# Upper half of z's rows by Strassen, first steps of the running sums on ScalarE

## The chip, the cores and the metric

One core of a Trainium2 chip. The time is device microseconds of one execution, the median over runs; what is compared is this time before and after the change. TensorE is called PE (its weight loads PEld), VectorE DVE, ScalarE ACT, GpSimd POOL, and SyncE SP. SP issues most transfers, POOL the indirect ones. Every engine executes its own list of instructions in order; waits between engines are semaphores.

## The reference

There are 32 batches of x, 512 channels by 1024 columns, float32, and one 512×512 matrix adj.

```python
# layer 0
q = wq . x;  k = wk . x                        # (B, N) each
att = softmax(leaky(q[:, None, :] + k[:, :, None]), axis=-1)   # slope 0.01
agg = einsum('bcn,bmn->bcm', x, att)
x = layernorm(x + relu(adj @ agg + bm))
# layer 1
W = adj * adj
x = layernorm(x + einsum('bnf,nm->bmf', x, W) + bias)
```

Both layernorms run over the last axis, 1024 elements.

## The kernel before, in words

**Layer 0.** The attention is not formed. A score is leaky(q_n + k_m), so for a given m the columns n fall into two sets by whether q_n exceeds −k_m, and in each set the weight is a product of a factor of q_n and one of k_m. The kernel therefore sorts the columns by q and takes running sums of z = xᵀ·adjᵀ (1024 rows of 512, one row per column n) with one weight upwards and another downwards. Each m then needs only one row of both tables, picked by its count.

In steps for batch b, with the words of the order lists: load x (`ld`); q and k rows by a small product (`parts` L223, copied by `parts_copy` L231, turned by `cols` L238); q's row goes to DRAM and back to all partitions (`row_out`, `row` L259); `row_max` (`rc`, L265); `rank` (`rk`, DVE, L275, 8 per batch) and `count` (`ct`, ACT, L288, 8 per batch). `product` (`z`, L314) makes 128 rows of z: for each j of 8, four matmuls of 128×128 by 128×512 into one PSUM bank; `product_copy` (`zc`, ACT, L320) takes them to `zt`, and `scatter` (`sc`, POOL, L328) writes them to sorted rows in DRAM. `sums_load` (`sl`) brings eight sorted rows to each partition, `sums_exp` (`se`, L352) makes the weights, `up` (`u`, L361 for j = 0, L366 after) and `down` (`d`, L374 for j = 7, L376 after) are the running sums on DVE, `carry` (`cu`, `cd`, L384) sums over partitions on PE with copies on ACT (L391), `table_up` and `table_down` (`tu`, `td`, L409) add the carries, and `table_write` (`tw`) writes the table to DRAM. `gather` (`g`, POOL, L436) picks rows, `mix_weights` (`mw`, L449), `mix_scale` (`ms`, ACT, L458) and `mix` (`mx`, DVE, L463) form the mean, `turn` (`t`, PE, L487) transposes it to channels by columns, and `residual` (`r`, DVE, L495) adds it to x. `spread0` (`s0`, ACT, L473), `root0`, `root0_end` (`rce`) and `norm0` (`n0`, ACT, L513) normalize the four channel tiles of x in place.

**Layer 1** is a product of the 512×512 matrix (adj∘adj plus the identity) with x, done for the quarters of both by the Strassen-Winograd form with seven products for eight. Sums of the matrix's quarters, S1 to S4, are made once in `weights` on POOL (L173–177). Sums of x's quarters are `T1` to `T4` (`t1`–`t4`, DVE, L524–538). The products are `U`, `V`, `Y`, `Z`, `C11`, `C12`, `C21` (PE, L545 and L580), two rows of tiles each; a running sum in one PSUM bank is copied out between them (`Uc`, `Vc`, `Zc`) and added back at the end (`upper` L600, `lower_right` L606, `lower_left` L613). `U` begins with a short pass that brings in the bias (L543). Then come the second normalization and the `store` (`st`).

**Buffers.** Four x tiles are in flight (`xp`). PSUM has four single banks (pool `p1`: z, q and k rows, carries, the sums of layer 1) and two pairs (pool `p2`: transposes, layer 1's pairs). `qb`, q's row on all partitions, has two buffers; the outputs `g` of layer 1 have four.

**Order.** The schedule is written by hand: three lists of words, `op.batch.index`, are emitted in order, and each engine gets its instructions in that order. `head` covers the start, `loop` is one period, in which one batch is in the products of z, the next in the running sums, one in the gathers and one in layer 1 (used for 15 values of b), `tail` covers the end. The framework adds semaphore waits where tiles or buffers overlap. A PSUM bank is one unit for it: a reader waits for all writes to the bank that were issued before it.

## Time and profile before

| | |
|---|---|
| median of 3 runs | 2003.04 us (2000.26 to 2005.85) |
| the profiled execution, own time | 2002.69 us |
| its span | 2001.0 us |
| mean granted PE clock | 0.988 |
| steady period (from U of one batch to U of the next) | 59.88 us |
| first U (layer 1 of batch 0) starts | 149.43 us |
| U of batch 28 starts | 1822.18 us |
| DMA, mean over the span | 279 GB/s |

The profile is of one execution. A line of the page's groups gives the code line, engine and operation, output and input by the program's names, and the count, then the busy time and the mean duration in ns; a line of the timeline gives start and length in us, and in brackets the idle time just before it and what ended it. Successive instructions overlap by a little, so durations add to more than the elapsed time; the rate of a run of equal instructions is read from the starts. A float32 matmul is recorded as two passes.

### The profile page before, as it was taken

Reading aid. Unit: us, or ns where it says so; the run is one execution under the profiler, and the core shown is the slowest. Engines: PE = TensorE matmul, PEld = TensorE weight load, DVE = VectorE, ACT = ScalarE, POOL = GpSimd, SP = SyncE. Lnnn points to the kernel's source line nnn. Section 1 sums busy time; section 2 is a strip of 40 time slices with the busy share of each in tenths; the row PEclk is TensorE's granted clock in tenths of the full one; section 3 lists DMA queues with packets and bytes.
Section 4 is the critical chain, followed back from the end, with each engine's and each line's share of the span. In section 5 each row is a group of like instructions: output and inputs, shape, how many; then the busy total and the mean of one; then the engine's idle time right before and its main releaser. Section 6 shows DMA issues by size and latency. Waiting matters only on the chain.

```text
span 2001.0 us, 21793 instructions
## 1 busy us (share of the span) xinstructions
PE 1937.7 (97%) x6353; PEld 939.7 (47%) x6353; DVE 1683.9 (84%) x2748; ACT 1512.4 (76%) x2560; POOL 870.7 (44%) x1090
## 2 busy tenths in 40 slices
PE   8979999999999999999999999999999999999866
PEld 4434444444444444444444444444444444444332
DVE  5888898898888888888888888888888889889662
ACT  3567788787788877788877788887778888777656
POOL 4333544434553434554444454444454443444331
PEclk9999999999999999999999999999999999999978
DMA  6677777877777877777877777877777877776742
GB/s 226 243 275 295 279 306 273 321 287 279 290 295 290 326 268 273 292 290 295 322 270 279 289 288 295 318 269 278 295 280 298 318 283 276 300 277 257 282 190 85
DMA packets 142832, 557.94 MB, mean 279 GB/s; under 512 B 15044, under 2 KB 15184, under 8 KB 134520
## 3 DMA queue, kind: packets, MB, share of 16 engines
q1 hardware_dynamic: 85328, 354.38, 46.7%
q0 software_dynamic: 57344, 202.15, 26.0%
q8 instruction: 50, 0.82, 0.2%
q14 instruction: 70, 0.57, 0.1%
q10 hardware_dynamic: 40, 0.02, 0.0%
HBM read 287.07 MB, written 269.42 MB: 278 GB/s over the span
## 4 chain that ended last, share of the span: by engine, by line
PE 78%; DVE 7%; DMA 7%; ACT 3%; issue 2%; POOL 2%; SPq 0%; POOLq 0%; DVEq 0%; ACTq 0%
PE z_ps L314 36%; PE sum_ps L545 18%; PE pair_ps L545 9%; PE pair_ps L580 4%; PE agg_ps L487 4%; PE qk_ps L223 3%; DMA got<-table,of 2%; DVE tab L409 2%; DMA tab<-sorted_z 1%; DMA sorted_z<-zt,to 1%; DVE junk_v L275 1%; PE carry_ps_False L384 1%; PE carry_ps_True L384 1%; ACT junk L473 1%; DVE x L495 1%
## 5 line engine op out<-in xcount | busy, mean ns | idle before, releaser
L314 PE MATMUL z_ps<-adj_t,x 128*128 128x512 f32 x2048 | 906.6, 594 | 0.0
L314 PEld LDWEIGHTS z_ps<-adj_t,x 128*128 128x128 f32 x2048 | 379.5, 190 | 444.8 <-issue 430.4
L436 POOL DMA_INDIRECT got<-table,of x256 | 289.7, 1132 | 467.1 <-PE z_ps L314 142.3
L328 POOL DMA_INDIRECT sorted_z<-zt,to x256 | 276.6, 1081 | 293.5 <-ACT zt L320 202.0
L275 DVE SCALAR_TENSOR_TENSOR junk_v<-qb,qkc,tie 128x1024 uint8<-128x1024 f32 x256 | 328.8, 1284 | 5.9
L288 ACT ACTIVATE junk_s<-qb,qkc 128x1024 uint8<-128x1024 f32 x256 | 294.0, 1148 | 6.0 <-DMA qb<-q_row 1.5
L636 ACT ACTIVATE g<-g,nb,tv 128x1024 f32<-128x1024 f32 x128 | 158.6, 1239 | 105.6 <-POOL nb L630 104.9
L320 ACT COPY zt<-z_ps 128x512 f32<-128x512 f32 x256 | 146.8, 577 | 91.2 <-PE z_ps L314 84.2
L480 POOL TENSOR_SCALAR tv<-tv 128x1 f32<-128x1 f32 x128 | 65.4, 511 | 333.1 <-ACT junk L473 330.3
L463 DVE SCALAR_TENSOR_TENSOR got<-got,w 128x512 f32<-128x512 f32 x256 | 184.3, 748 | 28.4 <-ACT got L458 28.3
L473 ACT ACTIVATE junk<-g,tv 128x1024 uint8<-128x1024 f32 x128 | 146.8, 1147 | 81.1 <-DVE g L600 51.1
L458 ACT ACTIVATE got<-got,w 128x512 f32<-128x512 f32 x256 | 165.9, 713 | 50.2 <-DVE w L453 49.9
L473 ACT ACTIVATE junk<-x,tv 128x1024 uint8<-128x1024 f32 x128 | 147.0, 1148 | 44.7 <-DVE x L495 39.4
L495 DVE SCALAR_TENSOR_TENSOR x<-agg_ps,small,x 128x1024 f32<-128x1024 f32 x128 | 161.0, 1280 | 18.5 <-PE agg_ps L487 18.5
L376 DVE SCALAR_TENSOR_TENSOR tab<-tab,ac 128x513 f32<-128x513 f32 x224 | 167.6, 748 | 0.4
L545 PE MATMUL sum_ps<-x,adj 128*128 128x512 f32 x256 | 129.0, 628 | 28.2 <-ACT x L513 28.2
L366 DVE SCALAR_TENSOR_TENSOR tab<-tab,ac 128x514 f32<-128x514 f32 x192 | 144.4, 752 | 12.3 <-ACT ac L352 7.9
L409 DVE TENSOR_TENSOR tab<-tab,carry 128x2052 f32<-128x2052 f32 x64 | 146.6, 2292 | 4.2 <-ACT carry L391 3.9
L487 PEld LDWEIGHTS agg_ps<-ident,got 128*128 128x128 f32 x1024 | 119.2, 143 | 40.4 <-issue 24.5
L513 ACT ACTIVATE x<-x,tv 128x1024 f32<-128x1024 f32 x128 | 136.5, 1136 | 2.0 <-DVE tv L509 1.9
L487 PE MATMUL agg_ps<-ident,got 128*128 128x128 f32 x1024 | 129.7, 277 | 7.3 <-DVE x L495 7.3
L409 DVE TENSOR_TENSOR tab<-tab 128x1539 f32<-128x1539 f32 x64 | 129.5, 2025 | 0.1
(119 smaller groups left out, 2606.4 us busy)
## 6 DMA issues: line engine op xcount, KB each, us to landing
table<-tab SPq DMA_DIRECT2D x64, 2056.0 KB
tab<-sorted_z SPq DMA_DIRECT2D x64, 1028.0 KB
x<-in_x_dram SPq DMA_DIRECT2D x128, 512.0 KB
out_dram<-g SPq DMA_DIRECT2D x128, 512.0 KB
qb<-q_row SPq DMA_DIRECT2D x32, 512.0 KB
sorted_z<-zt,to POOLq DMA_INDIRECT x256, 5.3
got<-table,of POOLq DMA_INDIRECT x256, 8.2
adj_in<-in_adj_dram SPq DMA_DIRECT2D x1, 1024.0 KB
```

Of the source, the lines that this page charges most:

```text
L275: nc.vector.scalar_tensor_tensor(junk, s.qb, s.q[:, j : j + 1], tie[:, at : at + N], ALU.subtract, ALU.is_gt, accum_out=s.rank[:, j : j + 1],)
L288: nc.scalar.activation(junk, s.qb, AF.Sign, bias=s.k[:, j : j + 1], accum_out=s.sign[:, j : j + 1])
L314: nc.tensor.matmul(s.z[j], xt[:, c, j * P : (j + 1) * P], adj_t[:, c, :], start=(c == 0), stop=(c == CT - 1),)
L328: nc.gpsimd.indirect_dma_start(out=sorted_z[b % 2][:, :], out_offset=bass.IndirectOffsetOnAxis(ap=s.to[:, j : j + 1], axis=0), in_=zt[:, j ...
L376: nc.vector.scalar_tensor_tensor(v, v, c, s.zs[:, j + 1, 0:D], ALU.mult, ALU.add)
L409: nc.vector.tensor_tensor(v, v, c, ALU.add)
L436: nc.gpsimd.indirect_dma_start(out=s.got[:, j, :], out_offset=None, in_=table[b % 2][:, :], in_offset=bass.IndirectOffsetOnAxis(ap=s.of[:, ...
L463: nc.vector.scalar_tensor_tensor(up, up, s.w[:, 0, j : j + 1], down, ALU.mult, ALU.add)
L473: nc.scalar.activation(junk, t, AF.Square, bias=v[0][:, i : i + 1], scale=-float(N), accum_out=v[1][:, i : i + 1],)
L487: nc.tensor.transpose(s.agg[o][:, j * P : (j + 1) * P], s.got[:, j, o * P : (o + 1) * P], ident)
L495: nc.vector.scalar_tensor_tensor(t[:, o, :], s.agg[o], nbm[:, o : o + 1], t[:, o, :], ALU.max, ALU.add, accum_out=s.v0[0][:, o : o + 1],)
L545: nc.tensor.matmul(ps, a[:, k, g * P : (g + 1) * P], v[:, k, :], start=False, stop=(k == 1), skip_group_check=first is None,)
```

## The change

Rows 0 to 511 of z (j = 0 to 3) are made as before. Rows 512 to 1023 are made by the Strassen-Winograd form of the 512×512 by 512×512 product xᵀ·adjᵀ: of the quarters of x's right half, x1 to x4 are four sums on DVE (128×512 elements each), R1 to R4 are the matching sums of adjᵀ's quarters, made once on POOL after S1 to S4. Seven products of 256×256 by 256×256 follow: zU, z11, zZ, zV, z12, zY, z21, each for k = 0 and 1, each two matmuls of 128×128 by 128×256. So 28 matmuls of 256 columns stand for 16 of 512.

The running sum z_sum of both k lies in one `p1` bank, 256 columns each; z_pair takes one `p2` buffer. Between the products ACT copies parts to `zt` (zUc, zVc, zZc, and z_lower_left, `zll`: eight copies of 128×256), and DVE adds PSUM to them (z_upper, `zup`, 128×512, twice; z_lower_right, `zlr`, 128×256, twice).

The first step of `up` and the first of `down` move from DVE to ACT. To make room, x1 to x4 share the buffers of layer 1's g_2 and g_3; `qb` has one buffer; the rank's throw-away output shares `end`; `part` and `carry` have one buffer of their own; T2, T3 and T4 lie in `zt` rows 0 to 1, 4 to 5 and 6 to 7. So z's rows j = 0 and 1 stay in PSUM until T4 is read. All three order lists are new; `head` now reaches to batch 12, and `loop` is used for 11 values of b.

```diff
-    op = ctx.enter_context(tc.tile_pool(name="op", bufs=CT))
+    op = ctx.enter_context(tc.tile_pool(name="op", bufs=1))
...
+    B11, B12 = adj_t[:, 0:2, 0:Q], adj_t[:, 0:2, Q:C]
+    B21, B22 = adj_t[:, 2:4, 0:Q], adj_t[:, 2:4, Q:C]
+    R1, R2, R3, R4 = [const.tile([P, 2, Q], F32, name=f"R{i}") for i in (1, 2, 3, 4)]
...
         nc.gpsimd.tensor_scalar(minus_A22, A22, -1.0, None, ALU.mult)
+        nc.gpsimd.tensor_tensor(R1, B12, B11, ALU.subtract)
+        nc.gpsimd.tensor_tensor(R2, B22, R1, ALU.subtract)
+        nc.gpsimd.tensor_tensor(R3, B22, B12, ALU.subtract)
+        nc.gpsimd.tensor_tensor(R4, B21, R2, ALU.subtract)
...
-        s.qb = sp.tile([P, N], F32, tag="qb", name=f"qb_{b}")
+        s.qb = one.tile([P, N], F32, tag="qb", name=f"qb_{b}")
...
+    def x_quarters(b):
+        t = xts[b]
+        return t[:, 0:2, H : H + Q], t[:, 2:4, H : H + Q], t[:, 0:2, H + Q : N], t[:, 2:4, H + Q : N]
+    def x_sums(b, i):
+        s, m = st[b], 2 + i // 2
+        if m not in s.xs:
+            t = op.tile([P, N], F32, tag=f"g{m}", name=f"x_sums_{b}_{m}")
+            s.xs[m] = t.rearrange("p (i k n) -> p i k n", i=2, k=2)
+        return s.xs[m][:, i % 2]
+    def x1(b):
+        _, _, X21, X22 = x_quarters(b)
+        nc.vector.tensor_tensor(x_sums(b, 0), X21, X22, ALU.add)
+    def x2(b):
+        nc.vector.tensor_tensor(x_sums(b, 1), x_sums(b, 0), x_quarters(b)[0], ALU.subtract)
+    def x3(b):
+        X11, _, X21, _ = x_quarters(b)
+        nc.vector.tensor_tensor(x_sums(b, 2), X11, X21, ALU.subtract)
+    def x4(b):
+        nc.vector.tensor_tensor(x_sums(b, 3), x_quarters(b)[1], x_sums(b, 1), ALU.subtract)
+    def z_quarter(ps, a, v, k, start, own):
+        for i in range(2):
+            nc.tensor.matmul(
+                ps, a[:, i, k * P : (k + 1) * P], v[:, i, :], start=start and i == 0,
+                stop=(i == 1), skip_group_check=not own,
+            )
+    def z_sum(b, k):
+        return st[b].zsum[:, k * Q : (k + 1) * Q]
+    def zU(b, k):
+        s = st[b]
+        start = s.zsum is None
+        if start:
+            s.zsum = p1.tile([P, C], F32, tag="m", name=f"z_sum_ps_{b}")
+        z_quarter(z_sum(b, k), x_quarters(b)[0], B11, k, start, start)
+    def zU_copy(b, k):
+        nc.scalar.copy(zt[:, 4 + k, 0:Q], z_sum(b, k))
+    def zV(b, k):
+        z_quarter(z_sum(b, k), x_sums(b, 1), R2, k, False, False)
+    def zV_copy(b, k):
+        nc.scalar.copy(zt[:, 4 + k, Q:C], z_sum(b, k))
+    def zY(b, k):
+        z_quarter(z_sum(b, k), x_sums(b, 2), R3, k, False, False)
+    def z11(b, k):
+        s = st[b]
+        if s.zpair is None:
+            s.zpair = p2.tile([P, N], F32, tag="w", name=f"z_pair_ps_{b}")
+        z_quarter(z_pair(b, k, 0), x_quarters(b)[1], B21, k, True, True)
+    def zZ(b, k):
+        z_quarter(z_pair(b, k, 1), x_sums(b, 0), R1, k, False, False)
+    def z12(b, k):
+        z_quarter(z_pair(b, k, 1), x_sums(b, 3), B22, k, False, False)
+    def z_upper(b, k):
+        v = zt[:, 4 + k, 0:C]
+        nc.vector.tensor_tensor(v, z_pair(b, k), v, ALU.add)
+    def z_lower_right(b, k):
+        v = zt[:, 6 + k, Q:C]
+        nc.vector.tensor_tensor(v, z_sum(b, k), v, ALU.add)
+    def z21(b, k):
+        z_quarter(z_sum(b, k), x_quarters(b)[3], R4, k, False, False)
+    def z_lower_left(b, k):
+        nc.scalar.copy(zt[:, 6 + k, 0:Q], z_sum(b, k))
...
-            nc.vector.tensor_scalar(s.up[0], s.zs[:, 0, :], s.ac[:, 0, 0:1], None, ALU.mult)
+            nc.scalar.activation(s.up[0], s.zs[:, 0, :], AF.Copy, scale=s.ac[:, 0, 0:1])
...
-            nc.vector.tensor_scalar(v, v, c, None, ALU.mult)
+            nc.scalar.activation(v, v, AF.Copy, scale=c)
...
-        s.T2 = one.tile([P, 2, H], F32, tag="T2", name=f"T2_{b}")
+        s.T2 = zt[:, 0:2, 0:H]
...
-        st[b].T3 = zt[:, 0:2, 0:H]
+        st[b].T3 = zt[:, 4:6, 0:H]
...
-        st[b].T4 = zt[:, 2:4, 0:H]
+        st[b].T4 = zt[:, 6:8, 0:H]
```

The middle of the new loop list, from the first product of z of one batch to the second U of layer 1 of the batch three before it:

```
z.0.0 ct.0.5 td.-2.1 s0.-3.3 ct.0.6 z.0.1 x1.0 tw.-2.1 ct.0.4 r.-3.0 ct.0.3 x2.0 rk.0.2
s0.-3.0 zU.0.0 x4.0 zU.0.1 ct.0.2 rk.0.7 z11.0.0 rt.-3 x3.0 z11.0.1 rk.0.1 zZ.0.0 zUc.0.1
zUc.0.0 rce.-3 zZ.0.1 ct.0.0 rk.0.0 g.-2.2 sl.-1.0 sl.-1.1 zV.0.0 zZc.0.1 rk.0.4 zZc.0.0
zV.0.1 zVc.0.0 n0.-3.1 z12.0.0 rk.0.3 g.-2.1 zVc.0.1 z12.0.1 n0.-3.2 zup.0.0 zY.0.1 zup.0.1
n0.-3.0 zY.0.0 rk.0.5 g.-2.0 ct.0.7 U.-3.0 zlr.0.1 t1.-3 n0.-3.3 g.-2.3 z21.0.1 se.-1.0
zlr.0.0 t2.-3 11.-3.0 g.-2.4 rk.0.6 zll.0.1 u.-1.0 z21.0.0 Uc.-3.0 u.-1.1 g.-2.6 ct.0.1
V.-3.0 re.0 u.-1.2 zll.0.0 u.-1.3 se.-1.1 sc.0.4 U.-3.1
```

## The prediction

> **What bounds the kernel now.** I read the page's busy times first, then the chain of work that ended last.
>
> ```profile
> span 2001.0 us, 21793 instructions
> PE 1937.7 (97%) x6353; PEld 939.7 (47%) x6353; DVE 1683.9 (84%) x2748; ACT 1512.4 (76%) x2560; POOL 870.7 (44%) x1090
> PE 78%; DVE 7%; DMA 7%; ACT 3%; issue 2%; POOL 2%; SPq 0%; POOLq 0%; DVEq 0%; ACTq 0%
> ```
>
> PE is busy for 97% of the span and is 78% of the last chain. An average hides stages, so next come windows of one period each (the columns are window, length, then busy time of PE, PEld, DVE, ACT and POOL, granted clock, DMA share, GB/s).
>
> ```profile
> 600.00:659.88 59.88, 59.88 (x199) 29.12 (x198) 52.17 (x85) 47.30 (x80) 26.75 (x33) 1.00 0.77 291
> 959.28:1019.16 59.88, 59.88 (x199) 29.12 (x198) 52.10 (x85) 47.30 (x80) 27.30 (x34) 1.00 0.76 291
> ```
>
> In the steady part PE never waits: 59.88 busy of 59.88, at full granted clock. DVE has 7.7 us over and ACT 12.6. So a microsecond off PE is a microsecond off the batch, as long as the others follow. The ends are different. The timeline shows the start:
>
> ```profile
> 19.30 1.67 POOL L177 TENSOR_SCALAR adj<-adj 128x512 f32<-128x512 f32 x1
> ...
> 31.78 1.22 DVE L265 TENSOR_REDUCE top<-qb 128x1 f32<-128x1024 f32 x1 [10.25 <-DMA qb<-q_row]
> ...
> 149.43 3.75 PE L545 MATMUL sum_ps<-x,adj 128*128 128x512 f32 x4 [10.82 <-ACT x L513]
> ```
>
> PE reaches the first U (layer 1 of batch 0) at 138.6 and waits 10.82 us for batch 0's x, so there PE is not the bound; the chain through DVE is. U of batch 28 starts at 1822.18 by the same view. The span thus divides into 149.43 + 28 × 59.74 + 178.8 us; the profiled execution's own time, 2002.69, is 1.7 above its span, and 0.35 below the median, 2003.04. I sum against 2002.69.
>
> **PE: what it removes and adds.** Sixteen matmuls of 512 columns per batch (z of j = 4 to 7) become 28 of 256 columns. The prices are in the timeline of one period (start, length; a group's starts give the rate, since ends overlap):
>
> ```profile
> 902.26 3.60 PE L314 MATMUL z_ps<-adj_t,x 128*128 128x512 f32 x8
> 905.70 1.04 PE L487 MATMUL agg_ps<-ident,got 128*128 128x128 f32 x8
> 906.57 3.60 PE L314 MATMUL z_ps<-adj_t,x 128*128 128x512 f32 x8
> ...
> 942.65 1.03 PE L384 MATMUL carry_ps_True<-end,before 128*128 128x257 f32 x4
> 943.52 1.88 PE L545 MATMUL pair_ps<-x,S 128*128 128x512 f32 x4
> ```
>
> A matmul is recorded as two passes. Eight passes of 512 columns take 905.70 − 902.26 = 3.44 us, 0.430 each; four passes of 257 take 943.52 − 942.65 = 0.87, 0.217 each. So 16 × 2 × 0.430 = 13.75 leaves and 28 × 2 × 0.215 (half of 0.430; 0.217 by the carry row) = 12.03 to 12.15 comes: 1.60 to 1.72 us less per batch. I take 1.72. Could short passes be held up by their weight loads, 0.190 each in the row of L384? The transposes of L487 run eight passes of 128 columns in 0.87, 0.109 each, with loads recorded at 0.143; so loads do not set the rate at 256 columns, and I price that at 0 to 0.1 us per batch. The Trainium skill, "TensorE: Matmul & The Clock Gate", section "Why this matters for your kernels", speaks against the change: for efficiency it wants all dimensions at 512 or more. The 257-column row runs at half the 512-column time and disagrees; by the rule the gain would be partly or wholly lost.
>
> **DVE.** Added per batch: four sums x1 to x4 of 128×512 from SBUF. The nearest rows are half a T1 (L524, 1.23 us for 128×1024: 0.61) and L463 (0.748 for two sources and a scalar); bounds 2.4 to 3.0, I take 2.5, as the operation is T1's own. Two z_upper of 128×512 from PSUM, as L606 at 0.68: 1.2 to 1.4. Two z_lower_right of 128×256: half that to 0.42 each: 0.7 to 0.85. Removed: u.0 (0.49, L361) and d.7 (0.48, L374). Net +3.4 to +4.3, taken as 3.6: 52.1 becomes 55.7 of some 58.5. All of it hides as long as DVE's waits, 7.7 per period now, shrink to 2.8.
>
> **ACT.** Four copies of 0.58 (L320) go, eight of 128×256 come at 0.36 (the row of L231), and two scalings at 0.71 (L458): −2.3 + 2.9 + 1.4 = +2.0, 49.3 of 58.5, hidden by 9 us of idle; but their place counts, see next.
>
> **New waits on PE.** z_sum's two halves share one PSUM bank, and the framework makes a reader wait for every earlier-issued write of that bank. So zVc.0 waits for the end of zV.1, though it reads zV.0's half. Behind it on ACT stand n0.1, zVc.1, n0.2 and n0.0, the normalized x that U waits for. ACT rows: copy 0.30 (two carry copies of L391 in 0.65), n0 1.07 (four of L513 in 4.27). From zV.1's end: 0.17 to start, then 0.30 + 1.07 + 0.30 + 1.07 + 1.07 = 4.0. PE has z12 and zY to do meanwhile, eight matmuls or 16 × 0.215 = 3.44, and U's bias pass, 0.21: it stalls about 0.35, or 0.45 with a hand-over of 0.1. zY.1 needs zVc.1 1.85 after zV.1's end and is reached at 1.72: part of the same stall. zlr.0 likewise waits for z21.1: DVE idles about 1 us there, and T2, which V needs, comes within 0.3 us of PE's need. U of row 1 needs the bank that zll.0 empties, behind u.0, Uc.0 and a count on ACT: on time by about 0.1. One stall of 0.45 and three near misses: I take 0.5 per batch, bounds 0 (the copies come early) and 1.7 (two more such stalls). The Trainium skill, "PSUM — Partial Sum Buffer", section "PSUM bank collisions raise a hardware error", asks for guards by bank, not by address, so these waits couldn't simply be dropped. No run here shows that; leaving the waits out would give 14 us less in the sum.
>
> **Moved or shared buffers.** x1 waits for the store of g_2, x4 for that of g_3, of the batch whose layer 1 has just ended: both issued before this batch's z in the lists, so 0, or up to 0.5 if the transfer lands late. q's row has one buffer instead of two, so its broadcast waits for the last count; behind it on SP stand the table writes: 0 to 0.6, hidden in DVE's wait. Table to gather to mix is a loop through DMA: td.0's end to the table landed 13.8, gathers to the mixing weights 13.2, mixing and transposes to the next sums about 26, carry and td.0 about 7: 59.9, exactly PE's period, since its links wait for PE; it shortens with PE and by u.0 leaving DVE. I price it at 0, upper bound 0.8.
>
> **Start.** R1 to R4 follow the S sums on POOL, idle from 20.97 on in before, at 1.45 each (L173): R2 at 24, R4 at 27. The first zV waits for R2. From 23.9, PE's list has seven groups of zV, zZ, zY and z21 (0.86 each), a full z (3.44), batch 1's q and k rows (1.86, L223) and a transpose (0.3) up to zY.1: 35.5. Both z_lower_right of batch 0 stand on DVE between that and row_max, with hand-overs 1.1: row_max moves from 31.8 to 36.6, +4.8. To batch 0's residual, DVE has 12 x sums (7.7), 6 z_upper (3.9) and 4 z_lower_right (1.5) more, and fewer ranks, running sums and table additions (about −9.3): some +3.8. U.0 then starts at 158.0, +8.6, with +3 to +17 as bounds.
>
> **Sum.** 158.0 + 28 × (59.74 − 1.72 + 0.50) + 178.8 = 158.0 + 1638.6 + 178.8 = 1975.4; with 1.7, **1977 us**. The tail, without products of z, is left as it is (±4).
>
> **Rivals.** (a) The gain is whole: PE finds the copies early and the start is absorbed, U.0 at 153. 153 + 28 × 58.02 + 178.8 + 1.7 = 1958. For it: DVE and ACT have room in every window. Against it: the chain behind zVc.0 is longer than its cover. (b) ACT's and DVE's near misses cost PE 1.2 a batch: 158 + 28 × 59.22 + 178.8 + 1.7 = 1997. (c) Slower: DVE becomes the bound. It executes in order, and its waits before are for others' results: the q columns' transposes 2.13, the gathers 1.29, count 1.28, the residual's transposes 0.70, T1's x 0.52 (timeline of one period). With 55.7 us of work, waits of 4.3 instead of 2.8 give a steady period of 60.0, a mean of 59.9 (59.74 stands for 59.88 before): 158 + 28 × 59.9 + 178.8 + 1.7 = 2016. It decides from waits of 3.9 on, where the mean passes 59.44 and the late start is no longer paid back (158 + 28 × 59.44 + 178.8 + 1.7 = 2003). For it: zlr adds a wait of 1 us, and batches gain DVE work of 3.6. Against it: waits for PE vanish when DVE is the later one. (d) The change doesn't do what it says: passes of 256 columns take up to 0.26 (carry's four with fill, 1.03/4). 28 × 2 × 0.26 = 14.6, +0.8 per batch: 158 + 28 × 61.0 + 178.8 + 1.7 = 2047. The L487 row excludes it almost.
>
> **How the numbers follow.** Chances: forecast (1967 to 1990) 0.54, (a) 0.12, (b) 0.17, (c) 0.13, (d) 0.04. A run of this kernel can't be told from no change within 0.3%, 6 us: 1997 to 2009. Faster takes the forecast, (a) and half of (b), 0.74; same, the rest of (b) and a little of (c), 0.11; slower, 0.15. The range reaches from below (a), 1956, into (c), 2010, leaving some 0.17 out: the bounds of the stall (0 to 1.7: 1963 to 2011) are nearly all within.
>
> **What would show it.** A steady window of 58.2 to 59.1 us with PE busy in all but about 0.5, that idle put down to ACT's n0 before U (L513); 28-matmul groups at 0.215 a pass; DVE about 55.7, ACT about 49.3 busy; U.0 at 153 to 165. I am wrong if PE idles over 1.4 us per period, if DVE shows no idle time, if a 256-column pass takes over 0.23, or if the first U comes after 170.

## The result and the profile after

| | before | after |
|---|---|---|
| median of 4 runs each, same chip | 2003.55 us (2000.26 to 2005.85) | 2031.62 us (2029.27 to 2037.12) |
| ratio, 95% interval | | 1.0145 (1.012 to 1.0171) |
| span of the profiled execution | 2001.0 | 2028.3 |
| mean granted PE clock | 0.988 | 0.981 |

The kernel became 1.45% slower, 28 us; the forecast was 1977 us, 27 us faster, with a range that ended at 2010. The page of the changed kernel, span, busy times and engines of the last chain:

```profile
span 2028.3 us, 23817 instructions
PE 1918.0 (95%) x7121; PEld 1077.6 (53%) x7121; DVE 1783.7 (88%) x2940; ACT 1553.3 (77%) x2750; POOL 875.2 (43%) x1085
PE 41%; DMA 13%; ACT 11%; DVE 8%; issue 5%; POOL 4%; SPq 1%; DVEq 0%; POOLq 0%; ACTq 0%
```

PE works 20 us less and the span is 27 us longer. PE's share of the chain that ended last fell from 78% to 41%: the time is now passed from engine to engine. Next, windows of the changed kernel (window, length, busy time of PE, PEld, DVE, ACT and POOL, granted clock, DMA share, GB/s): the period at the same place as before, then the ten periods after the first U, the eleven periods of the loop list, and the start up to the first U.

```profile
959.28:1019.16 59.88, 59.10 (x221) 32.57 (x220) 54.30 (x92) 48.20 (x85) 26.91 (x34) 1.00 0.78 291
168.50:783.72 615.22, 590.03 (x2209) 332.28 (x2207) 551.82 (x912) 480.92 (x854) 270.08 (x332) 0.99 0.76 288
783.72:1442.00 658.28, 651.89 (x2444) 365.51 (x2443) 604.06 (x1002) 535.74 (x947) 303.25 (x364) 1.00 0.78 291
0.00:168.50 168.50, 136.53 (x558) 84.15 (x559) 131.18 (x213) 84.23 (x166) 62.14 (x79) 0.95 0.52 199
```

Per loop period that is 59.84 us, PE busy for 59.26, DVE for 54.91, ACT for 48.70. No engine is full, and the period is what it was. To see where the time lies I cut both spans at the starts of U of batches 0, 10, 21 and 28 (the timeline of PE) and set against each stage what its passes take by themselves: 0.430 us for one of 512 columns, 0.215 for 256, and so on. The rest of the stage is lost to PE.

| stage | before: length, lost | after: length, lost | forecast length |
|---|---|---|---|
| start to U.0 | 149.4, 22.8 | 168.5, 47.1 | 158.0 |
| U.0 to U.10 | 595.8, 7.8 | 615.2, 41.0 | 583.6 |
| U.10 to U.21, the loop list | 659.4, 5.1 | 658.3, 22.9 | 646.0 |
| U.21 to U.28 | 417.6, 4.6 | 427.7, 21.7 | 409.1 |
| U.28 to the end | 178.8, 55.8 | 158.6, 45.9 | 178.8 |
| sum | 2001.0, 96.1 | 2028.3, 178.6 | 1975.5 |

(Forecast lengths: those of before with 1.22 us less per period.) PE's passes come to 1904.9 us before and 1849.7 after: 55.2 less, where 32 times 1.72 are 55.0. The saving is all there. But PE loses 82.5 us more, in every stage but the last. The last gained 20 us, half of it (10.3) because 24 passes of z, at 0.430 each, stood behind U.28 in before and now stand ahead of it; why PE loses 9.9 less there as well is not shown.

The busy time hides most of such a loss: PE's recorded idle time in the loop grew by 6.3 us (659.40 − 659.27 = 0.13 before, 658.28 − 651.89 = 6.39 after), while the starts show 17.8. A stall inside a group, and the slower passes behind it, are counted as busy. Rates must be read from starts.

**The saving.** The timeline of one period of the changed kernel, PE's new products (start, length, line, output and input, count):

```profile
1072.54 1.89 PE L359 MATMUL z_sum_ps<-adj_t,x 128*128 128x256 f32 x8
1074.26 1.89 PE L359 MATMUL z_pair_ps<-adj_t,x 128*128 128x256 f32 x8
1075.99 1.89 PE L359 MATMUL z_pair_ps<-R,x_sums 128*128 128x256 f32 x8
```

From start to start, eight passes take 1.72 us: 0.215 each, as forecast, with their weight loads hidden.

**The largest single loss.** The timeline around 190 us, PE and then DVE (in brackets the idle time before, and what ended it):

```profile
193.69 2.08 PE L481 MATMUL carry_ps_True<-end,before 128*128 128x257 f32 x4 [12.36 <-DVE end L463]
197.79 8.94 PE L642 MATMUL sum_ps<-zt,S 128*128 128x512 f32 x16 [2.02 <-DVE zt L626]
206.56 1.88 PE L642 MATMUL sum_ps<-zt,adj 128*128 128x512 f32 x4
```

```profile
179.55 2.33 DVE L463 SCALAR_TENSOR_TENSOR tab<-tab,ac 128x514 f32<-128x514 f32 x3 [5.63 <-ACT tab L458]
188.08 0.17 DVE L546 TENSOR_TENSOR w<-bd,got 128x8 f32<-128x8 f32 x1 [6.19 <-DMA got<-table,of]
```

PE's list has the carry of batch 2's running sums (`cu.2`) before the rest of batch 0's layer 1. DVE makes these sums, and waits twice itself: 5.63 us for their first step, u.0, which is now on ACT (L458) and stands there, with the weights that it needs, behind copies of layer 1; and 6.19 us for batch 1's gathered rows, since the mixing weights (L546) stand on DVE ahead of the last steps of the sums. PE idles for 12.36 us. The next four passes take 2.08 for 0.87, the sixteen from 197.79 on 8.77 for 6.88, and in between T2 (L626) is late by 2.02. Together 12.36 + 1.21 + 2.02 + 1.89 = 17.5 us, nearly half of what PE loses in this stage. The long passes are the clock: windows of this stretch show it at half and then 0.78.

```profile
193.69:195.77 2.08, 2.08 (x4) 1.17 (x4) 1.79 (x6) 0.72 (x1) 0.77 (x1) 0.50 1.00 372
197.79:206.00 8.21, 8.21 (x15) 3.63 (x16) 6.59 (x11) 4.05 (x9) 0.77 (x2) 0.78 0.45 162
```

The Trainium skill, "TensorE: Matmul & The Clock Gate", section "What's actually happening", states this: after an idle window of some 3.4 us the clock is halved until PE has been busy that long. The 0.50 agrees.

**The loop's losses** are small and many. Put down by starts, the 22.9 us of eleven periods are: x's load, ahead of the last quarter of the q and k rows, 4.9 (what these groups take above the 1.86 us of before); ACT's copies of z_sum, zUc (L379) ahead of zV 3.9 and zVc (L385) ahead of zY 2.3; the rest in smaller pieces for layer 1 (ahead of V, which needs T2, 1.7 and ahead of U, which needs the normalized x, 1.6, each with the slow passes behind it), in passes that restart slowly (2.3 in zV and zY), and in the group of q and k rows, whose price per pass is set a little low here (before has that too). The view of PE's waits over these periods (waiting line, what it waited for, us in total, times, longest) has only part of this:

```profile
PE qk_ps L232 <- DMA x<-in_x_dram: 2.6, 7, 0.8
PE z_sum_ps L359 <- ACT zt L379: 2.6, 4, 1.0
PE sum_ps L642 <- DVE g L703: 0.5, 1, 0.5
```

In the period whose products are shown above, zUc comes late because it stands on ACT behind `root0` (L602), whose table load takes 1.28 us:

```profile
1075.67 1.28 ACT L602 ACT_TABLE_LOAD   x1
```

Next, the load of x in a period of before, and in one after (SP issues, PE uses):

```profile
1005.35 1.77 SPq L87 DMA_DIRECT2D x<-in_x_dram  x4
...
1013.79 1.93 PE L223 MATMUL qk_ps<-x,wqk 128*32 128x256 f32 x32
```

```profile
984.62 1.77 SPq L87 DMA_DIRECT2D x<-in_x_dram  x4
...
991.78 1.50 PE L232 MATMUL qk_ps<-x,wqk 128*32 128x256 f32 x24
...
993.52 0.64 PE L232 MATMUL qk_ps<-x,wqk 128*32 128x256 f32 x8 [0.24 <-DMA x<-in_x_dram]
```

Before, PE asked for x 8.44 us after the issue, and it was there. After, it asks 7.16 us after the issue, and the last quarter is late. In other periods it asks after 7.3 to 7.6 us. SP issues the load when T4 (DVE, L635) has read the x buffer: T4 ends at 984.53, the issue is at 984.62.

### The profile page after: what moved, and what is told of

Its sections match the earlier page's. It is cut to its first block, busy times and chain, and to the rows that moved or that the text cites. A ratio compares the mean times of both kernels' runs of the same rounds, so it can differ in the third digit from the quotient of the medians.

```text
span 2028.3 us, 23817 instructions
## 1 busy us (share of the span) xinstructions
PE 1918.0 (95%) x7121; PEld 1077.6 (53%) x7121; DVE 1783.7 (88%) x2940; ACT 1553.3 (77%) x2750; POOL 875.2 (43%) x1085
## 4 chain that ended last, share of the span: by engine, by line
PE 41%; DMA 13%; ACT 11%; DVE 8%; issue 5%; POOL 4%; SPq 1%; DVEq 0%; POOLq 0%; ACTq 0%
PE z_ps L324 10%; PE sum_ps L642 10%; PE z_sum_ps L359 6%; DMA got<-table,of 6%; PE pair_ps L642 4%; DMA x<-in_x_dram 4%; PE z_pair_ps L359 3%; PE agg_ps L584 3%; PE pair_ps L677 2%; ACT junk L570 2%; DMA qb<-q_row 2%; ACT junk_s L298 2%; ACT got L555 2%; ACT x L610 1%; POOL tv L578 1%
## 5 line engine op out<-in xcount | busy, mean ns | idle before, releaser
L324 PE MATMUL z_ps<-adj_t,x 128*128 128x512 f32 x1024 | 459.9, 596 | 3.1 <-ACT zt L330 1.4
L425 POOL DMA_INDIRECT sorted_z<-zt,to x256 | 294.0, 1149 | 277.3 <-ACT zt L330 75.7
L324 PEld LDWEIGHTS z_ps<-adj_t,x 128*128 128x128 f32 x1024 | 188.5, 190 | 214.4 <-issue 206.1
L642 PE MATMUL sum_ps<-zt,S 128*128 128x512 f32 x512 | 239.5, 602 | 5.6 <-DVE zt L626 5.0
L555 ACT ACTIVATE got<-got,w 128x512 f32<-128x512 f32 x256 | 167.6, 713 | 67.9 <-DVE w L550 67.8
L642 PEld LDWEIGHTS sum_ps<-zt,S 128*128 128x128 f32 x512 | 96.8, 192 | 123.3 <-issue 104.8
L577 POOL TENSOR_SCALAR tv<-tv 128x1 f32<-128x1 f32 x128 | 60.0, 469 | 205.9 <-ACT junk L570 201.7
L359 PE MATMUL z_sum_ps<-R,x_sums 128*128 128x256 f32 x512 | 130.8, 390 | 15.8 <-POOL R L182 7.1
L610 ACT ACTIVATE x<-x,tv 128x1024 f32<-128x1024 f32 x128 | 142.3, 1147 | 0.9 <-DVE tv L606 0.9
```

The lines of the kernel that those rows point to most:

```text
L324: nc.tensor.matmul(s.z[j], xt[:, c, j * P : (j + 1) * P], adj_t[:, c, :], start=(c == 0), stop=(c == CT - 1),)
L359: nc.tensor.matmul(ps, a[:, i, k * P : (k + 1) * P], v[:, i, :], start=start and i == 0, stop=(i == 1), skip_group_check=not own,)
L425: nc.gpsimd.indirect_dma_start(out=sorted_z[b % 2][:, :], out_offset=bass.IndirectOffsetOnAxis(ap=s.to[:, j : j + 1], axis=0), in_=zt[:, j ...
L555: nc.scalar.activation(down, down, AF.Copy, scale=s.w[:, 1, j : j + 1])
L642: nc.tensor.matmul(ps, a[:, k, g * P : (g + 1) * P], v[:, k, :], start=False, stop=(k == 1), skip_group_check=first is None,)
```

## The experiments

Three theories stood against each other. By the first, the changed kernel is held by **the order and the buffers**: new results that PE, ACT and DVE hand to each other, buffers shared between batches. By the second, rival (c), **DVE's work** (or ACT's) is the bound. By the third, **the table's loop** is: table to DRAM, gathers, mixing, running sums, next table, which in before had the same length as PE's period and through which DMA moves most of its bytes. Ratios are to the kernel before, timed beside each run on the same chip; its medians there were 2003.8 to 2008.9.

### PE's saving by itself, and the table's loop

e1 leaves before as it is, order, buffers and all, and gives z's upper rows the same 28 matmuls of 256 columns, and nothing else.

```diff
-        for c in range(CT):
+        for c in range(CT if j < 4 else 0):
...
+        for m in range(7 if j >= 4 else 0):
+            h, c = m // 4, m % 4
+            nc.tensor.matmul(
+                s.z[j][:, h * Q : (h + 1) * Q], xt[:, c, j * P : (j + 1) * P],
+                adj_t[:, c, h * Q : (h + 1) * Q],
+                start=(m == 0), stop=(m in (3, 6)), skip_group_check=(h == 1),
```

> The kernel before, with one edit: for j = 4 to 7 each z takes 7 matmuls of 256 columns (four for the left half of adj's columns, three for the right) in place of 4 of 512, so PE does exactly the 28 short matmuls per batch of the changed kernel, and nothing else of the change is there (no sums, no copies, no new waits, the old lists). The right half of these rows of z lacks the last 128 channels. Theory 1, PE's saving is real and what surrounds it gave it back: a steady period of 58.2 us in place of 59.88 and 2003.5 - 28 x 1.7 = 1955 us (1950 to 1966). Rival, the loop through table, gather and mixing is as long as PE's period and holds it at 59.9: 1995 to 2003 us, with PE idle some 1.5 us per period.

2000.75 us, ratio 0.9974 (0.9965 to 0.9984). 5 us of a possible 55. The loop's period is 59.68. Its last chain and a window over the eleven periods (same columns as above):

```profile
PE 39%; DMA 20%; DVE 17%; ACT 10%; issue 7%; POOL 4%; SPq 1%; DVEq 0%; POOLq 0%; ACTq 0%
```

```profile
748.40:1404.90 656.50, 649.52 (x2444) 367.50 (x2443) 573.69 (x936) 515.53 (x881) 302.21 (x363) 1.00 0.77 292
```

So before had a second limit, 0.2 us below PE's period. PE was busy in all of 59.88 us in before and still was not what a shorter product pays for. Not all of the missing 50 us lies there: e1's first U comes at 155.8, 6.4 us later than in before, and what follows it is 8.7 us shorter. In or just behind the q and k rows of batch 3, between 113 and 120 us, PE stands still for nothing that the profile names, and the clock is at 0.50 from 117.5 to 124.4; e5 and e7 below show the same (first U at 155.2 and 156.5), e18 does not (151.5). The cause isn't known.

To see whether the second limit is the table's transfer, e5 is e1 with half of each table's rows written from batch 2 on, and e6 the changed kernel with the same edit.

```diff
-        at = slice(4 * h, 4 * h + 4)
+        at = slice(4 * h, 4 * h + (4 if b < 2 else 2))
```

> e1 (the kernel before with PE's 28 short matmuls), and from batch 2 on only half of each table write (rows j = 0, 1 and 4, 5 of each partition; the others keep what batch b - 2 wrote, so gathered rows are partly another batch's): 2.1 MB instead of 4.2 per batch and some 7 us less between the end of the running sums and the gathers. e1 ran at 2000.8 with PE idle, its chain going from table_down through the table write, the gathers, the mixing and the running sums to the next table_down. Theory 2, that loop holds the period at 59.5 to 59.9 beside PE: with it shorter, PE's 58.2 shows, 1950 to 1965. Rival, PE's waits in e1 come from elsewhere (x's load, the order of the lists): within 8 us of 2001.

> The changed kernel with the same halved table writes from batch 2 on (the gathered rows partly another batch's). Theory 2, the loop through table, gathers, mixing and running sums bounds the changed kernel: the steady period falls from 59.84 to 58.2 to 58.8 and the head's +19 shrinks, 1985 to 2005. Rival 1b, PE's short waits for ACT's copies and x's load bound it by themselves: period 59.6 or more, time 2020 to 2032.

e5: 1973.58, ratio 0.9825 (0.9808 to 0.9841). e6: 2040.15, ratio 1.0148 (1.013 to 1.0166). With the table's loop shortened, PE's saving in before's order is there: a period of 58.60, and PE busy in nearly all of it.

```profile
915.70:974.30 58.60, 58.45 (x223) 33.51 (x223) 51.95 (x86) 47.07 (x81) 27.23 (x34) 1.00 0.70 261
```

In the changed kernel the same edit gives nothing. The table's loop was the second limit of before; it is not what holds the changed kernel.

e7 and e8 take traffic away elsewhere: only a quarter of each output row is stored, in e1 and in the changed kernel.

```diff
-        nc.sync.dma_start(out=out[b, m * P : (m + 1) * P, :], in_=st[b].g[m])
+        nc.sync.dma_start(out=out[b, m * P : (m + 1) * P, 0:Q], in_=st[b].g[m][:, 0:Q])
```

> e1 with only a quarter of each output row stored (256 of 1024 columns; the rest of the output is left out): 1.6 MB less per batch of transfers that stand in no loop between batches. If the loop through the table is long because its transfers share the DMA engines with others (0.77 busy in the mean), its transfers get shorter and the time falls by 10 to 40 us; if it is long by its own issue, latency and engine steps, or PE's waits come from elsewhere, within 5 us of 2001.

> The changed kernel with only a quarter of each output row stored (the rest of the output is left out): 1.6 MB less per batch on the DMA engines, no engine's work and no loop between batches shortened in any other way (the stores' buffers come free sooner). If shared DMA time is what stretches the table loop and x's load (0.57 us per period of PE's wait), the time falls by 15 to 45 us from 2032; if not, within 6 us of it.

e7: 1997.04, ratio 0.9944 (0.9927 to 0.996). e8: 2030.05, ratio 1.0104 (1.0087 to 1.0121). 0.3 to 0.4% in either. A batch stores 1.6 MB less this way, and writes 2.1 MB less with half tables, which gave e1 1.5%. From 800 to 1400 us the DMA engines are busy for 0.77 in e1, 0.71 in e7 and 0.70 in e5: at nearly the same relief of traffic only the shorter table loop lets PE's saving through. It is the table's own way that counts there, more than traffic as such.

### One part of the change at a time

e2 puts u.0 and d.7 back on DVE; e3 leaves the sums x1 to x4 out, and the products read x's quarters; e4 makes R1 to R4 before the S sums.

```diff
-            nc.scalar.activation(s.up[0], s.zs[:, 0, :], AF.Copy, scale=s.ac[:, 0, 0:1])
+            nc.vector.tensor_scalar(s.up[0], s.zs[:, 0, :], s.ac[:, 0, 0:1], None, ALU.mult)
...
-            nc.scalar.activation(v, v, AF.Copy, scale=c)
+            nc.vector.tensor_scalar(v, v, c, None, ALU.mult)
```

> The changed kernel with the first steps of both running sums put back on DVE (0.49 + 0.48 us per batch), off ACT. Theory 1a, DVE's work bounds the changed kernel: its period grows by about 0.9, 59.84 to 60.7, and the time by 25 us to 2057. Theory 1b, a ring of short waits through ACT (the copies between the small products, u's first step ahead of the copies that free banks) bounds it: ACT is relieved by 1.4 us per batch and the time falls by 5 to 20 us, to 2012 to 2027. Neither: within 5 us of 2031.

```diff
-        s, m = st[b], 2 + i // 2
...
-        return s.xs[m][:, i % 2]
+        return x_quarters(b)[i]
...
+    x2 = x3 = x4 = x1
```

> The changed kernel without the four sums of x's quarters: the products read the plain quarters in their place, so rows 512 to 1023 of z are other numbers; the DVE work (2.5 us per batch) and the waits of these sums for the stores of g_2 and g_3 go, PE's work and all other waits stay. Theory 1a, DVE's work bounds: the period falls from 59.84 to PE's own 58.2 to 58.6, the head recovers, time 1965 to 1985. Theory 1b, PE's short waits on ACT's copies and on x's load bound it: these stay, 1.3 to 1.6 us per period, and the time falls by 5 to 15 only, to 2016 to 2026.

```diff
+        nc.gpsimd.tensor_tensor(R1, B12, B11, ALU.subtract)
+        nc.gpsimd.tensor_tensor(R2, B22, R1, ALU.subtract)
+        nc.gpsimd.tensor_tensor(R3, B22, B12, ALU.subtract)
+        nc.gpsimd.tensor_tensor(R4, B21, R2, ALU.subtract)
...
-        nc.gpsimd.tensor_tensor(R1, B12, B11, ALU.subtract)
-        nc.gpsimd.tensor_tensor(R2, B22, R1, ALU.subtract)
-        nc.gpsimd.tensor_tensor(R3, B22, B12, ALU.subtract)
-        nc.gpsimd.tensor_tensor(R4, B21, R2, ALU.subtract)
```

> The changed kernel with R1 to R4 made on POOL before adj squared and S1 to S4, not behind them. In the changed kernel PE waited 7.1 us for R2 at 17.5 us, and the first U came at 168.5 where I had 158. If that wait is on the chain to the first U, U comes 4 to 7 us earlier and the time falls by as much, to 2025 to 2028; if what comes after it at the start (DVE's backlog, z_lower_right behind products) sets the first U, under 2 us.

| | us | ratio | U.0 | loop period |
|---|---|---|---|---|
| after | 2031.62 | 1.0145 (1.012 to 1.0171) | 168.5 | 59.84 |
| e2, steps on DVE | 2046.36 | 1.021 (1.019 to 1.0229) | 168.7 | 60.37 |
| e3, no sums of x | 2034.16 | 1.0133 (1.0115 to 1.0151) | 168.9 | 59.92 |
| e4, R first | 2034.81 | 1.0145 (1.0128 to 1.0162) | 167.6 | 60.13 |

Moving the steps to ACT is a good part of the change, worth about 0.65%; and with the steps back on DVE the ten periods after U.0 take 615.9 us for 615.2 and the stall is still 11.54 us, with DVE waiting 6.19 us for the weights (ACT, L449). So it is the weights on ACT that are late there, not u.0's new engine. The sums of x cost nothing: taking 2.2 us of DVE's busy time per batch out (54.91 to 52.70 in the loop) changes neither the period nor the start. That speaks against rival (c). The R sums on POOL aren't the start's price either: without PE's wait of 7.13 us for R2, it waits 6.23 for the second sum of x.

### Undoing single waits

e9 splits the x tile in two halves with buffers of their own; the first half of x is loaded behind T3 and not behind T4. e10 uses the loop list from the first batch on instead of the head. e11 reorders the loop list around z_sum's bank: zUc ahead of root0, zVc.0 before zV.1, both zlr before z21.1, two counts later. e12 is all three.

```diff
-    mx.-2.1 sc.0.6 mx.-2.2 u.-1.7 Z.-3.1 Zc.-3.0 g.-2.5 t3.-3 d.-1.7 mx.-2.0 V.-3.1 sc.0.7
+    mx.-2.1 sc.0.6 mx.-2.2 u.-1.7 Z.-3.1 Zc.-3.0 g.-2.5 t3.-3 lf.1 d.-1.7 mx.-2.0 V.-3.1 sc.0.7
```

> The changed kernel with each x tile kept as two tiles of two channel rows each, and in the loop list (13 turns' worth of it, 11 used) the first half's load issued right behind T3, ahead of C12 and T4, which read only the second half. Theory 3, a ring through all engines holds the changed loop at 59.84: x's load (9.3 us from issue to landing), q and k rows, z and its Strassen products on PE up to z21, then z_lower_right, T2, the running sums and mixing weights on DVE up to T4 (17 us without a gap), which frees x's buffer for the next load; no engine is full, and taking work out where the ring runs elsewhere (e3, e6) moves nothing. Half of x landing some 4 us earlier shortens it: period 58.8 to 59.3 in the loop's 11 turns, 2032 to 2020 to 2026. Rival 1b, PE's wait for x (0.57 per period) is one of several independent waits: the same 6 to 8 us, but then all other waits stay as they are. If neither: within 4 us.

```diff
-    emit(head, 0)
-    for b in range(13, 24):
-        emit(loop, b)
...
+    emit("ld.1 bias.0 ld.2 ld.3", 0)
+    for b in range(-1, 24):
+        emit(part_of(loop, b), b)
```

> The changed kernel with the head list left out: the loop list is used from the first batch on (words of batches below 0 dropped, the first four loads issued at once), so only the order of the first 13 periods is new. After's loss stands in the first periods: the first U at 168.5 instead of 149.4, and ten periods of 61.5 instead of 59.6. Theory 4, it is the order written for them, a serial zig-zag between engines, not work: the first U comes by 155 and every period takes some 59.8, 155 + 28 x 59.8 + 159 + 2 = 1990, below the kernel before. If the changed work itself can't be done faster from a cold start: 2025 to 2040.

```diff
-    s0.-3.0 zU.0.0 x4.0 zU.0.1 ct.0.2 rk.0.7 z11.0.0 rt.-3 x3.0 z11.0.1 rk.0.1 zZ.0.0 zUc.0.1
-    zUc.0.0 rce.-3 zZ.0.1 ct.0.0 rk.0.0 g.-2.2 sl.-1.0 sl.-1.1 zV.0.0 zZc.0.1 rk.0.4 zZc.0.0
-    zV.0.1 zVc.0.0 n0.-3.1 z12.0.0 rk.0.3 g.-2.1 zVc.0.1 z12.0.1 n0.-3.2 zup.0.0 zY.0.1 zup.0.1
...
+    s0.-3.0 zU.0.0 x4.0 zU.0.1 rk.0.7 z11.0.0 zUc.0.1 zUc.0.0 rt.-3 ct.0.2 x3.0 z11.0.1 rk.0.1
+    zZ.0.0 rce.-3 zZ.0.1 rk.0.0 g.-2.2 sl.-1.0 sl.-1.1 zV.0.0 zZc.0.0 zZc.0.1 zVc.0.0 n0.-3.1
+    rk.0.4 z12.0.0 zV.0.1 rk.0.3 g.-2.1 zVc.0.1 z12.0.1 n0.-3.2 zup.0.0 zY.0.1 zup.0.1 n0.-3.0
```

> The changed kernel with its loop list reordered around the shared PSUM bank, nothing else: zUc ahead of root0's table load, zVc.0 between zV.0 and zV.1 with z12.0 as cover, both z_lower_right before z21.1, two counts later. Takes away PE's waits for zUc and zVc (0.56 per period with their restarts) and DVE's wait for z21 (0.95). Theory 3, the ring contains both: the period falls by 0.8 to 1.5 to 58.4 to 59.0, time 2032 to 2016 to 2024 (11 turns). Rival, x's load or another loop holds 59.8 and PE waits there instead: within 4 us of 2032, with PE's wait for x's load grown to 1 us or more.

> e9, e10 and e11 together: x in two halves, the reordered loop list, used from the first batch on. If the three causes are separate, their gains add: first U by 155, period 58.3 to 58.8, 155 + 28 x 58.6 + 159 + 2 = 1957, faster than both kernels by over 2 per cent. If one ring only takes the place of another: 1985 or more.

| | us | ratio | U.0 | U.0 to U.10 | loop period |
|---|---|---|---|---|---|
| after | 2031.62 | 1.0145 (1.012 to 1.0171) | 168.5 | 615.2 | 59.84 |
| e9, x in halves | 2078.96 | 1.034 (1.032 to 1.0361) | 170.1 | 622.8 | 62.35 |
| e10, loop from the start | 2030.84 | 1.0108 (1.0091 to 1.0125) | 176.9 | 604.1 | 60.06 |
| e11, loop reordered | 2044.41 | 1.0171 (1.0145 to 1.0198) | 169.2 | 617.0 | 60.69 |
| e12, all three | 2062.47 | 1.0258 (1.0227 to 1.0289) | 174.3 | 611.6 | 61.12 |

All three missed. In each the wait it was made for went, or shrank, and another took its place. In e9, PE no longer waits for x. Its timeline shows why the period grew (T4 on DVE, then PE in the same period):

```profile
1002.06 1.23 DVE L655 TENSOR_TENSOR zt<-zt,x 128x1024 f32<-128x1024 f32 x1 [3.02 <-DMA sorted_z<-zt,to]
```

```profile
1006.90 3.70 PE L662 MATMUL sum_ps<-zt,adj 128*128 128x512 f32 x8 [1.75 <-DVE g L723]
```

T4 lies in rows 6 and 7 of `zt`, so it waits until the scatters have read z there. With x's transfer begun earlier, these reads end later (a scatter lands 5.0 us after its issue, the median in the loop, for 4.0 in the changed kernel; that the load is what delays them is inferred, not shown). DVE stands still for some 2.2 us per period, and lower_right (L723), behind T4 on DVE, is late for PE's `21`. In e11 the list of PE's waits over the loop reads (waiting line, what it waited for, us in total, times, longest):

```profile
PE z_sum_ps L359 <- ACT zt L417: 10.3, 11, 0.9
PE qk_ps L232 <- DMA x<-in_x_dram: 6.4, 9, 1.7
```

Here z21.0 waits in every period for the copy zll.1 (L417) of the other half of its bank, where the changed kernel waits for zUc and zVc. e10 takes away the stall of 12 us: from U.0 to U.10 PE loses 26.5 us for 41.0. But U.0 comes 8.4 us later, and ahead of it PE now waits 9.8 and 5.3 us for DVE at two of these carries: the stall moved, and the head list had bought an earlier U.0 with it.

### Engines relieved

What if each engine besides PE gets room? e13 lets the counts read 256 of q's 1024 columns (in the loop ACT is busy for 43.9 us per period instead of 48.7), e14 mixes 256 of 512 columns (DVE 52.9 instead of 54.9).

```diff
-            junk, s.qb, AF.Sign, bias=s.k[:, j : j + 1], accum_out=s.sign[:, j : j + 1]
+            junk[:, 0:Q], s.qb[:, 0:Q], AF.Sign, bias=s.k[:, j : j + 1], accum_out=s.sign[:, j : j + 1]
```

> The changed kernel with each count over the first 256 of 1024 columns (the counts, and so the gathered rows, are others): some 0.8 us less for each of 8 on ACT, 6 us per batch, in the stretch where its copies of z's parts and n0 stand. Theory 5, the changed loop is a ring in which ACT, DVE and PE are each full in turn, and PE waits behind ACT's copies: the loop's period falls from 59.84 to PE's 58.2 to 59.0 and the first U comes earlier by 5 or more: 2032 to 1990 to 2010. Rival, ACT is only a bystander (49 of 60 us busy) and DVE with the gathers holds it: within 8 us of 2032.

```diff
-        up, down = s.got[:, j, 0:C], s.got[:, j, ZR : ZR + C]
+        up, down = s.got[:, j, 0:Q], s.got[:, j, ZR : ZR + Q]
```

> The changed kernel with each mix on DVE over 256 of 512 columns (half of each mixed row is left as gathered): 8 x 0.33 = 2.6 us less DVE work per batch, all of it in the stretch between z_lower_right and the carry, where DVE runs without a gap; e3 took 2.5 us of DVE work from the stretch before it and gained nothing. Theory 5: this stretch is in the ring, period down by 1 to 1.6, time 2032 to 1995 to 2015. If DVE's work holds nothing: within 6 us of 2032.

e15 is the changed kernel with the edits of e3, e6, e13 and e14 together; e16 is before with the half table, the short counts and the half mix; e17 is e15 with x in halves as in e9; e18 is e1 (PE's saving in before's order) with the edits of e16.

> The changed kernel with all that could stand beside PE made shorter at once: no sums of x's quarters (e3), half table writes (e6), short counts (e13), half mix (e14); PE's work unchanged. What is left is PE's work and the order: if the order lists and PE's copies-and-waits are sound, PE is full at 58.2 per period, 1945 to 1965. If the waits between the short products hold PE by themselves, whatever the other engines' work: 1985 or more.

> The kernel before with the same relief (half table writes, short counts, half mix), as the measure for e15: PE was full at 59.88 without it, so the steady part stays and only the first U (its 10.8 us wait) and the end may come earlier: 1975 to 2000. e15 less e16 is what the change's PE saving is worth with the others out of the way: by PE's passes alone -48 us (28 x 1.72).

> e15 (the changed kernel with its other engines relieved; 2016, loop period 59.6 with PE waiting 0.84 per period for x's load) with x in two tiles, the first half loaded ahead, as in e9. In e9 the wait for x went, but T4 waited 2.2 us per period for the scatters that read its place in zt. If with lighter transfers that does not come back, PE's waits in the loop shrink to the copies' (about 0.6): period 58.7 to 59.0, time 2005 to 2010. If another wait takes its place again: within 4 us of 2016, or above.

> e1 (the kernel before with PE's 28 short matmuls, old order, none of the new dependencies) with the relief of e16 (half table writes, short counts, half mix). PE should be full at 58.16 in every steady period: 1995.7 - 28 x 1.7 = 1948 (1944 to 1956). It has the same PE passes as e15, which ran at 2016 with the same relief; what is between them, some 68 us, is then the order and the dependencies of the Strassen form alone. If e18 stays above 1970, the short passes themselves cost more than their columns.

| | us | ratio | U.0 | U.0 to U.10 | loop period | PE lost in the loop |
|---|---|---|---|---|---|---|
| e13, after, short counts | 2026.99 | 1.0114 (1.0091 to 1.0137) | 167.3 | 615.4 | 59.59 | 22.5 |
| e14, after, half mix | 2028.14 | 1.0115 (1.0092 to 1.0138) | 168.7 | 611.0 | 60.02 | 27.2 |
| e15, after, all relief | 2016.39 | 1.0059 (1.0042 to 1.0076) | 168.1 | 612.4 | 59.61 | 22.7 |
| e16, before, relief | 1995.65 | 0.9955 (0.9939 to 0.9972) | 149.1 | 594.7 | 59.88 | 6.8 |
| e17, e15 with x in halves | 2067.33 | 1.0309 (1.0281 to 1.0337) | 170.2 | 619.0 | 62.20 | 48.8 |
| e18, e1 with relief | 1961.97 | 0.9793 (0.9777 to 0.9809) | 151.5 | 582.0 | 58.60 | 9.2 |

Windows over the eleven periods of e15, and of e18:

```profile
780.50:1436.20 655.70, 647.92 (x2432) 367.01 (x2443) 557.01 (x958) 484.03 (x947) 285.02 (x363) 1.00 0.71 256
```

```profile
733.40:1378.00 644.60, 643.55 (x2443) 368.74 (x2443) 551.11 (x936) 462.29 (x881) 291.86 (x364) 1.00 0.70 262
```

These two have the same 28 short matmuls, and DVE's and ACT's work is alike (50.6 and 44.0 us per period in e15, 50.1 and 42.0 in e18). In before's order PE loses 0.8 us per period and the period is 58.60; in the new order it still loses 2.1, although DVE has 9 us over. 2016 against 1962: 54 us (53 by the ratios) are the price of the new order, the new hand-overs and the shared buffers together, without anybody's work being the bound. With room for the others, PE's saving is worth 1995.65 − 1961.97 = 34 us (32 by the ratios). e17 missed as e9 did: with the lighter transfers T4's wait for the scatters is the same, 25.9 us in its eleven periods.

## Why the prediction was wrong

**Right in size.** "0.215 (half of 0.430)": measured 0.215, and 55.2 us less work for PE. DVE "55.7": 54.91. ACT "49.3": 48.70. No added operation was mispriced in the loop: a sum of x 0.69, z_upper 1.29 for two, z_lower_right 0.42, a copy 0.26 from start to start. Rival (d), slow short passes, is out. The tail is another matter: "without products of z … left as it is (±4)", it came out 20 us shorter: before had 24 passes of z in it, 10.3 us, which moved ahead of it. That was luck: the four other stages came out 73 us longer than forecast, and the tail gave 20 back.

**First failed step: "Table to gather to mix is a loop through DMA … 59.9, exactly PE's period, since its links wait for PE; it shortens with PE … I price it at 0, upper bound 0.8."** It does not shorten with PE. e1 shows it: the same saving with nothing else changed gives 0.2 us per period instead of 1.72, and with the table's transfer halved, e5, 1.3. That the loop was as long as PE's period was a warning, and I read it as a consequence. This isn't what holds the changed kernel (e6), but with the old order it takes all but 0.2 us of the period's gain.

**Second failed step: "One stall of 0.45 and three near misses: I take 0.5 per batch, bounds 0 (the copies come early) and 1.7".** From starts, PE loses 2.1 us per loop period for 0.5 before. Of the places named, zVc ahead of zY costs 0.21 per period, the place ahead of V (T2) 0.15 and the one ahead of U (the normalized x), which was to be the stall, 0.14; the bank that zll.0 empties costs nothing. The two largest were not in the list: x's load with 0.45, and zUc ahead of zV with 0.35. I had gone through the buffers that the change shares, and not through the time that the load still has between T4 and the q and k rows, 0.8 to 1.3 us less, nor through what stands on ACT ahead of zUc. None of the signs of being wrong came: PE's recorded idle time was 0.58 per period, DVE was idle for 4.9, a short pass took 0.215, the first U came at 168.5. The first was set on recorded idle time, and that hides most of the loss.

**Third failed step: "158.0 + 28 × (59.74 − 1.72 + 0.50)", the loop's price taken for all periods.** Only 12.3 us of the miss lie in the eleven periods of the loop list. 31.6 lie between U.0 and U.10, 18.6 between U.21 and U.28, in the two lists that were rewritten as much as the loop and that I did not walk through. One wait, cu.2's, is 17.5 us.

**Fourth: the start, "+8.6, with +3 to +17 as bounds".** It is +19.1: +10.4 up to row_max for "+4.8", and +8.7 from there for "+3.8". R2's time held (zV.0 at 24.64, for "24"). Row_max was put at 36.6 and came at 42.20, since zlr.1 stands ahead of it on DVE and waits for two ACT copies and PE's order, as DVE's timeline shows:

```profile
38.07 0.42 DVE L411 TENSOR_TENSOR zt<-z_sum_ps,zt 128x256 f32<-128x256 f32 x1 [8.80 <-PE z_sum_ps L359]
41.78 0.43 DVE L411 TENSOR_TENSOR zt<-z_sum_ps,zt 128x256 f32<-128x256 f32 x1 [3.28 <-ACT zt L417]
...
42.20 1.21 DVE L274 TENSOR_REDUCE top<-qb 128x1 f32<-128x1024 f32 x1
```

e3 and e4 (first U at 168.9 and 167.6) show that the sums are worth nothing there and R's place 0.9 us. From 42.2 on, there are waits of the same kind (PE waits 4.10 us for ACT's copy of z at 139.57, and 4.80 for zlr at 163.95); their shares in the 8.7 us weren't separated. With short passes and none of the new order the first U already comes at 151.5 to 156.5 (e18, e5, e1, e7).

**Rival (c)** named the side and, with 60.0, nearly the period (59.84); its 2016 us are half of the loss. But its mechanism, DVE as the bound, is wrong: DVE waits 4.9 us per period, and e3, e14 and e15 take 2.1 to 4.3 us of its busy time away for 0.2 us at most in the period. That is a nearly right period for a wrong reason.

**Open.** Which of the new hand-overs would have to go, and in which order, for the new form to reach e18's period: three attempts only moved the waits. Buffers of their own for T2 and T4 would cut the tie between layer 1 and the scatters; there is no room for them in this kernel, and it wasn't tried. No kernel that computes the whole came out faster than before.

## What to carry to other kernels

An engine that is busy in all of its period may share that length with a second loop; shorten the engine's work alone, with nothing else changed, and see whether the period follows, before paying for a form that needs a new order. A form that saves work on the bound by cutting it into pieces with copies and sums between them turns one long independent run into a chain of hand-overs over three engines: price the chain in every list that is rewritten, head and tail too, and each transfer by the time that it has left, not only by what it moves.

## What the runs showed of the hardware

**A pause of PE costs more than its length.** After 12.36 us of idle time the clock stood at 0.50, and the 20 passes behind it took 3.1 us more than at full clock. After 7.13 us, before zV.0, four short passes took 1.87 us for 0.86.

**DVE and POOL hold each other up.** A sum of two tiles of 128×512 takes 0.69 us on DVE in the loop. At the start, while POOL made R1 to R4, the first took 0.67 and the second 1.64 (POOL's timeline, then DVE's):

```profile
20.91 2.01 POOL L181 TENSOR_TENSOR R<-adj_t 128x512 f32<-128x512 f32 x1
21.13 0.67 DVE L345 TENSOR_TENSOR x_sums<-x 128x512 f32<-128x512 f32 x1
21.83 1.64 DVE L348 TENSOR_TENSOR x_sums<-x_sums,x 128x512 f32<-128x512 f32 x1
```

POOL's own R1, beside the first, took 2.01 us, where the S sums of the same size took 1.33 to 1.60. The Trainium skill, "SBUF — State Buffer", section "Who interferes with whom", says that a DVE instruction with two SBUF inputs contends with a GpSimd instruction that reads SBUF; these rows agree. In the loop POOL has little arithmetic, and the sums ran at full speed.
